# Self-attention layers of a four-layer transformer kernel: tied transposes, 4 KB pieces, later products, and one pair in eight transposed by TensorE

## The chip, the cores and the metric

The kernel runs on one core of a Trainium2 chip. That core has five engines which work side by side, each through its own list of instructions, strictly in order: TensorE (PE; its loads of weights are listed apart as PEld), VectorE (DVE), ScalarE (ACT), GpSimd (POOL) and SyncE (SP), which mostly issues DMAs. The metric is the device time of one execution in microseconds. Lower is better.

## The reference

x is (4, 1024, 256): four items of 1024 tokens with 256 channels, all in fp32. Four layers follow one another: L0 (16 heads: self-attention, cross-attention to a context of 77 tokens, feed-forward), L1 (three attention blocks of 4 heads with 64 channels each), L2 and L3 (16 heads, cross-attention). The change concerns the second and third blocks of L1, where queries, keys and values all come from x. Cut to what matters:

```python
Q = relu(q @ Wq + bq);  K = relu(k @ Wk + bk);  V = relu(v @ Wv + bv)   # (4,1024,256), 4 heads of 64
scores = einsum('hbqd,hbkd->hbqk', Qh, Kh) / sqrt(64)                   # 1024 x 1024 for each head
scores = where(key_mask == 0, NEG, scores)
attn = softmax(scores, axis=-1) * query_mask
out = layer_norm(einsum('hbqk,hbkd->hbqd', attn, Vh) + q)
enc = leaky_relu(out @ Wff + bff, 0.2) + out                            # q, k, v of the next block
```

## The kernel before

**Units.** The class Self4 computes such a block for one item. Two blocks times four items make eight items, and each has 16 units: p = 0, 1 (a pair of heads) times t = 0 to 7 (a tile of 128 queries). The 128 units fill 948 to 1902 us of the profiled execution, "the stage" here. One unit consists of the following.

- *Scores* (scores, L1262): four matmuls (eight records) of 64x512 give 128 queries x 1024 keys for each of two heads, in two PSUM tiles named ss. Their pool has two buffers, so a unit's ss tiles are the only ones: the next unit's scores can write only what this unit's exponentials have read.
- *Reductions* (L1273): VectorE takes the maximum over the keys, one reduction for each head.
- *Exponentials* (L1279): ScalarE writes exp(score - max) for both heads into a tile PR and sums it in passing. One PR holds a pair of units, that is two query tiles (t even, t odd). There are two PR buffers.
- *Block transposes* (turned_by_blocks, L1291): the products with V need the probabilities with keys on the partitions. VectorE transposes PR in place in blocks of 32x32, one instruction of 128x2048 for a unit. It is called one unit later (pipe.later("next", 1)).
- *The DMAs* (L1298): after the pair's second block transpose, 16 DMAs of 128 KB each move the blocks from PR to a tile PT, where the whole is transposed. Half is issued by SP (a = 0, 2), half by POOL (a = 1, 3); each DMA consists of runs of 1 KB. There are two PT buffers.
- *Products with V* (weighted, L1334): 16 matmuls of 128x256 for each half of the keys, called at ("turn", 2) and ("turn", 3): the first half two units after the DMAs were issued, the second half one unit after that. After the second half ScalarE copies the result from PSUM into OT (carry, L1512). For every four query tiles, OT is transposed back and normalized (normal, L1348).
- *A step of the pump*: work for the neighbouring items, spread evenly over the units. It consists of the heads of Q and K (L1226, L1231; evicted by ScalarE into QK, L1233), of V (values, L1187, L1190; evicted by ScalarE in L1194), of turns of x (L1167, L1396; copied by ScalarE, L1512), and of the feed-forward (L1402, L1405; ScalarE in L1410, then VectorE in L1411 and L1412).

**Order.** TensorE's order is written by hand: it is the order in which Pipe.unit calls the parts, and the call of a kind that was deferred ("full", "next", "turn", "late", "col") stands where its name stands there:

```python
        self.call("full")
        if scores:
            scores()
        self.call("next")
        self.now += cost
        self.pump()
        for kind in ("turn", "late", "col"):
            self.call(kind)
```

So TensorE does scores, step, products in each unit. The orders of the other engines are made when the kernel is built, by a planner that estimates when each instruction could start; `issue_after` ties an instruction behind a given one.

**Branches.** What the mask holds selects a branch at run time. In the branch that runs here `net.blocks` is true: PR and PT take two buffers of 16 KB a partition each, and `carry` is always a ScalarE copy.

## Time and profile before

| | us |
|---|---|
| median of 3 runs | 2405.5 |
| the three runs | 2398.03, 2405.5, 2406.79 |
| the profiled execution | 2396.79 |
| its span | 2394.9 |
| mean granted TensorE clock | 0.958 |
| the stage of the 128 units | 948 to 1902 |

The profiled execution is one run of the program; its time is the metric's, and its span runs from the first to the last instruction. In the profile's rows, L12 stands for line 12 of the kernel. A group row reads: line, engine, operation, written tile <- read tile, size, count, then busy time in us and mean ns of one, then the engine's idle time just before these instructions and what ended most of it. A row of waits reads: engine, tile and line that waited <- what it waited for: us in total, times, longest. A timeline row reads: start in us, length in us, engine, line, operation, tiles, size, count, and in brackets the idle time before and its releaser. PEclk and "clock" are the TensorE clock that was granted, as a share of full speed.

### The profile page before, as it was taken

How to read it: one execution, taken by the hardware profiler on the slowest of the kernel's cores; microseconds unless marked ns; L12 is line 12 of the kernel's file. 1: busy time of each engine (PE TensorE's matmuls, PEld its weight loads, DVE VectorE, ACT ScalarE, POOL GpSimd, SP SyncE). 2: the span in 40 equal slices, each digit the busy share in tenths (PEclk: the TensorE clock that was granted, in tenths of full speed). 3: DMA queues.
4: the chain of work that ended last, by engine and by line, in shares of the span. 5: the costliest groups of instructions: out<-in, count | busy, mean ns of one | idle time of the engine just before them, and what ended most of it. 6: DMA issues, size and time to landing. Idle time of an engine off the chain costs nothing. (4 is left out here: it accounts for less than half of the span.)

```text
span 2394.9 us, 31195 instructions
## 1 busy us (share of the span) xinstructions
PE 2204.3 (92%) x11035; PEld 1204.8 (50%) x11035; DVE 1582.6 (66%) x3167; ACT 930.2 (39%) x1828; POOL 380.4 (16%) x648
## 2 busy tenths in 40 slices
PE   6899999999898979999999899999999899999996
PEld 3565446566577655545454445454545344444442
DVE  6665553534424565888888788888888656656765
ACT  2222332222232355545454454444444234434333
POOL 2000000000000000333333233333333100000000
PEclk8999989989998998999999999999999899999988
DMA  5000010000000000667776577766787400000000
GB/s 147 1 3 14 5 36 1 1 3 5 12 1 7 1 5 1 146 147 152 151 156 144 123 151 157 151 142 141 148 163 143 97 5 1 5 1 1 27 18 28
DMA packets 148677, 158.01 MB, mean 66 GB/s; under 512 B 51432, under 2 KB 130849, under 8 KB 148513
## 3 DMA queue, kind: packets, MB, share of 16 engines
q1 hardware_dynamic: 122161, 85.63, 17.2%
q0 software_dynamic: 25296, 69.24, 13.1%
q8 instruction: 91, 1.49, 0.3%
q10 hardware_dynamic: 1056, 1.05, 0.1%
q14 instruction: 73, 0.60, 0.1%
HBM read 17.41 MB, written 4.19 MB: 9 GB/s over the span
## 5 line engine op out<-in xcount | busy, mean ns | idle before, releaser
L1279 ACT ACTIVATE PR<-ss,nm 128x1024 f32<-128x1024 f32 x256 | 284.7, 1114 | 366.2 <-DVE nm L1273 290.2
L1291 DVE STREAM_TRANSPOSE PR<-PR 128x2048 f32<-128x2048 f32 x128 | 295.8, 2311 | 128.9 <-ACT PR L1279 114.3
L1298 POOL DMA_DIRECT2D PT<-PR x512 | 279.6, 554 | 577.7 <-PE ss L1262 236.7
L1262 PE MATMUL ss<-QK 64*128 64x512 f32 x1024 | 324.8, 628 | 28.8 <-ACT PR L1279 28.5
L1273 DVE TENSOR_REDUCE nm<-ss 128x1 f32<-128x1024 f32 x256 | 299.6, 1210 | 13.8 <-PE ss L1262 13.8
L377 ACT ACTIVATE PT<-pb 77x1024 f32<-77x1024 f32 x192 | 185.4, 1015 | 193.2 <-PE pb L373 193.2
L1334 PE MATMUL po<-PT,V 128*64 128x256 f32 x2048 | 251.1, 387 | 5.1 <-DMA PT<-PR 5.1
L281 DVE TENSOR_REDUCE mx<-pa 128x4 f32<-128x308 f32 x384 | 161.4, 470 | 83.7 <-PE pa L276 82.5
L1262 PEld LDWEIGHTS ss<-QK 64*128 64x128 f32 x1024 | 113.3, 187 | 176.8 <-ACT PR L1279 99.7
L1334 PEld LDWEIGHTS po<-PT,V 128*64 128x64 f32 x2048 | 136.6, 137 | 108.4 <-issue 51.1
L276 PE MATMUL pa<-KA,QT 64*128 64x308 f32 x768 | 169.1, 486 | 14.0 <-DVE mx L281 12.8
L1545 POOL TENSOR_TENSOR pw<-va,minus_half 128x4 f32<-128x4 f32 (+1 forms) x28 | 38.8, 1384 | 714.5 <-DVE va L1543 542.0
L386 PE MATMUL po<-PT,Vc 77*32 77x512 f32 x768 | 140.4, 639 | 7.6 <-ACT PT L377 7.0
L276 PEld LDWEIGHTS pa<-KA,QT 64*128 64x128 f32 x768 | 84.3, 193 | 99.1 <-issue 37.0
L604 PE MATMUL pp<-hF,w 128*128 128x256 f32 x512 | 116.9, 382 | 0.0
L367 PE MATMUL pb<-QT,KA 32*77 32x512 f32 x768 | 114.1, 665 | 0.0
L619 PE MATMUL pp<-w,hid 128*128 128x256 f32 x512 | 113.7, 379 | 0.0
L619 PEld LDWEIGHTS pp<-w,hid 128*128 128x128 f32 x512 | 97.0, 190 | 16.5 <-issue 2.2
L604 PEld LDWEIGHTS pp<-hF,w 128*128 128x128 f32 x512 | 95.6, 190 | 18.2 <-issue 6.0
L266 PE MATMUL pp<-hT,wq 128*128 128x512 f32 x192 | 98.0, 646 | 5.5 <-ACT hT L1507 5.0
L1536 DVE BATCH_NORM_STATS2 st<-x 128x6 f32<-128x256 f32 x256 | 97.7, 403 | 3.2 <-DMA x<-in_x 2.3
L1405 PE MATMUL pp<-wo,hE 128*128 128x256 f32 x384 | 96.4, 393 | 1.6 <-ACT hE L1512 1.6
(256 smaller groups left out, 3079.5 us busy)
## 6 DMA issues: line engine op xcount, KB each, us to landing
PT<-PR SPq DMA_DIRECT2D x512, 128.0 KB
PT<-PR POOLq DMA_DIRECT2D x512, 128.0 KB, 4.9
x<-in_x SPq DMA_DIRECT2D x4, 1024.0 KB
out<-x SPq DMA_DIRECT2D x8, 512.0 KB
w<-in_ff_w SPq DMA_DIRECT2D x2, 1024.0 KB
gb<-in_norms POOLq DMA_DIRECT2D x5, 256.0 KB, 6.6
wk<-in_l_wk SPq DMA_DIRECT2D x10, 128.0 KB
wv<-in_l_wv SPq DMA_DIRECT2D x5, 256.0 KB
```

Of the source, the lines that this page charges most:

```text
L276: nc.tensor.matmul(pas[i], self.qt[rows, e, ts(t, P)], self.ka[rows, e, :, :], start=True, stop=True)
L281: nc.vector.tensor_reduce(out, pas[i].rearrange("p (j s) k -> p j s k", s=2), AX.X, ALU.max, negate=True)
L377: nc.scalar.activation(pt[:, 2 * i : 2 * i + 2, :], pbs[i][:SC], AF.Exp, scale=self.l.scale)
L386: nc.tensor.matmul(po[ts(j, h.slot), :], l.v[:, self.b, col : col + h.vw], pt[:, j, :], start=True, stop=True)
L604: nc.tensor.matmul(pp[:, i, :], self.w1[:, cc, ts(f + i, P)], s["hT"][:, cc, ts(q, 2 * P)], start=cc == 0, stop=cc == NC - 1)
L619: nc.tensor.matmul(pp[:, u, :], s["a"][:, f, ts(u, P)], self.w2[:, f, :], start=f == 0, stop=f == NF - 1)
L1262: nc.tensor.matmul(ss[h][:, k, :], self.qk[p][rows, 0, ts(t, P)], self.qk[p][rows, 1, ts(k, 512)], start=True, stop=True,)
L1273: nc.vector.tensor_reduce(self.nm[:, t, at], s2, AX.X, ALU.max, negate=True)
L1279: nc.scalar.activation(out, s2, AF.Exp, bias=self.nm[:, t, at], accum_out=self.sums[:, t, at])
L1291: nc.vector.transpose(part, part)
L1298: (nc.sync, nc.gpsimd)[a % 2].dma_start(out=pt[ts(c, 32), :, :, a].rearrange("p t h k j -> p (t h) (k j)"), in_=pr[ts(a, 32), :, :, ts(c, ...
L1334: nc.tensor.matmul(po[64 * h : 64 * h + 64], self.v[:, k, 64 * (2 * p + h) : 64 * (2 * p + h) + 64], pts[:, :, h, :, k, :] if net.blocks e ...
```

## The change

Four edits in Self4, all for the branch in which `net.blocks` is true.

1. Each block transpose is tied behind the later reduction of the scores issued last (`net.reduced`), which is the second reduction of the next unit.
2. PR and PT get another layout, so that each of the 16 DMAs moves runs of 4 KB in place of 1 KB. POOL issues the DMAs with a = 3 alone, SP those with a = 0, 1, 2.
3. The products with V move from ("turn", 2 + half) to ("next", 3 + half): a unit later, and ahead of the unit's pump step, so that TensorE does scores, products, step.
4. The pair of units with p = 1 and t = 2, 3 of each item (one pair in eight) skips the block transposes and the DMAs. Its probabilities are written in plain order, and `turned` transposes them on TensorE: 16 transposes of 128x128 for each of the two units, both sets called in one unit, with a ScalarE copy (carry) of 128x512 from PSUM to PT after every four.

```diff
--- before.py
+++ after.py
@@ -1263,22 +1263,27 @@
                     ss[h][:, k, :], self.qk[p][rows, 0, ts(t, P)], self.qk[p][rows, 1, ts(k, 512)],
                     start=True, stop=True,
                 )
+        blocks = net.blocks and (p, t // 2) != (1, 1)
         if not net.blocks:
             pr = net.tile("E", [P, 2, S], name="PR")
         elif t % 2 == 0:
-            self.pr = net.tile("E", [P, 2, 2, S], name="PR")
+            self.pr = net.tile("E", [P, 4, 2, 2, S // 4], name="PR")
+        if net.blocks and not blocks:
+            pr = self.pr.rearrange("p c t h n -> p (c t h n)")[:, ts(t % 2, 2 * S)].rearrange("p (h n) -> p h n", h=2)
         for h in range(2):
             at = slice(2 * p + h, 2 * p + h + 1)
             s2 = ss[h].rearrange("p k n -> p (k n)")
-            nc.vector.tensor_reduce(self.nm[:, t, at], s2, AX.X, ALU.max, negate=True)
-            if net.blocks:
-                out = self.pr[:, t % 2, h, :].rearrange("p (c k i) -> p k c i", c=4, i=32)
+            net.reduced = nc.vector.tensor_reduce(self.nm[:, t, at], s2, AX.X, ALU.max, negate=True)
+            if blocks:
+                out = self.pr[:, :, t % 2, h, :].rearrange("p c (k i) -> p k c i", i=32)
                 s2 = s2.rearrange("p (k c i) -> p k c i", c=4, i=32)
             else:
                 out = pr[:, h, :]
             nc.scalar.activation(out, s2, AF.Exp, bias=self.nm[:, t, at], accum_out=self.sums[:, t, at])
-        if net.blocks:
+        if blocks:
             net.pipe.later("next", 1, lambda pr=self.pr: self.turned_by_blocks(p, t, pr))
+        elif net.blocks:
+            net.pipe.later(("next", "turn")[t % 2], 2 - t % 2, lambda: self.turned(p, t, pr))
         else:
             net.pipe.later("full", 1, lambda: self.turned(p, t, pr))
 
@@ -1287,21 +1292,22 @@
 
         net = self.net
         nc = net.nc
-        part = pr[:, t % 2].rearrange("p h s -> p (h s)")
-        nc.vector.transpose(part, part)
+        part = pr[:, :, t % 2].rearrange("p c h n -> p c (h n)")
+        with net.tc.issue_after(net.reduced.ins):
+            nc.vector.transpose(part, part)
         if t % 2 == 0:
             return
 
-        pt = net.tile("B", [P, 2, 2, 4, NT, 32], name="PT")
+        pt = net.tile("B", [P, 4, 2, 2, NT, 32], name="PT")
         for c in range(4):
             for a in range(4):
-                (nc.sync, nc.gpsimd)[a % 2].dma_start(
-                    out=pt[ts(c, 32), :, :, a].rearrange("p t h k j -> p (t h) (k j)"),
-                    in_=pr[ts(a, 32), :, :, ts(c, 256)].rearrange("p t h n -> p (t h) n"),
+                (nc.gpsimd if a == 3 else nc.sync).dma_start(
+                    out=pt[ts(c, 32), a].rearrange("p t h k j -> p (t h k j)"),
+                    in_=pr[ts(a, 32), c].rearrange("p t h n -> p (t h n)"),
                 )
         state = []
         for half in range(2):
-            net.pipe.later("turn", 2 + half, lambda half=half: self.weighted(p, t, pt, half, state))
+            net.pipe.later("next", 3 + half, lambda half=half: self.weighted(p, t, pt, half, state))
 
     def turned(self, p, t, pr):
 
@@ -1315,25 +1321,26 @@
                 pm = net.p1.tile([P, 4, P], F32, tag="p1", name="pm")
                 for i in range(4):
                     nc.tensor.transpose(pm[:, i, :], pr[:, h, ts(k + i, P)], net.ident)
-                net.evac(pts[:, t % 2, h, k : k + 4, :], pm)
+                net.carry(pts[:, t % 2, h, k : k + 4, :], pm)
         if t % 2:
             state = []
             for half in range(2):
-                net.pipe.later("col", half, lambda half=half: self.weighted(p, t, pts, half, state))
-
-    def weighted(self, p, t, pts, half, state):
+                when = ("next", 3 + half) if net.blocks else ("col", half)
+                net.pipe.later(*when, lambda half=half: self.weighted(p, t, pts, half, state, False))
+
+    def weighted(self, p, t, pts, half, state, blocks=True):
         net = self.net
         nc = net.nc
         if half == 0:
             state.append(net.p1.tile([P, 2, P], F32, tag="p1", name="po"))
         po = state[0]
-        if net.blocks:
+        if blocks:
             po = po.rearrange("p t (a j) -> p t a j", a=4)
         for k in range(4 * half, 4 * half + 4):
             for h in range(2):
                 nc.tensor.matmul(
                     po[64 * h : 64 * h + 64], self.v[:, k, 64 * (2 * p + h) : 64 * (2 * p + h) + 64],
-                    pts[:, :, h, :, k, :] if net.blocks else pts[:, :, h, k, :], start=k == 0, stop=k == NT - 1,
+                    pts[:, :, :, h, k, :].rearrange("p a t j -> p t a j") if blocks else pts[:, :, h, k, :], start=k == 0, stop=k == NT - 1,
                 )
         if half:
             if t % 4 == 1:
```

## The prediction

> **What bounds the kernel now.** First the page's engine totals and slices, then the self-layer stage alone, then who waits for whom in it, then single units. "Scores", "products", "exponentials" and "step" are used as above; s is the start of a unit's first scores matmul.

> ```profile
> PE 2204.3 (92%) x11035; PEld 1204.8 (50%) x11035; DVE 1582.6 (66%) x3167; ACT 930.2 (39%) x1828; POOL 380.4 (16%) x648
> L1279 ACT ACTIVATE PR<-ss,nm 128x1024 f32<-128x1024 f32 x256 | 284.7, 1114 | 366.2 <-DVE nm L1273 290.2
> L1291 DVE STREAM_TRANSPOSE PR<-PR 128x2048 f32<-128x2048 f32 x128 | 295.8, 2311 | 128.9 <-ACT PR L1279 114.3
> q1 hardware_dynamic: 122161, 85.63, 17.2%
> q0 software_dynamic: 25296, 69.24, 13.1%
> ```

> The windows view for 948 to 1902 us (columns: length; busy us of PE, PEld, DVE, ACT, POOL; clock; DMA share; GB/s), then the waits:

> ```profile
> 948.00:1902.00 954.00, 901.14 (x4382) 444.31 (x4380) 789.16 (x1023) 446.73 (x912) 300.59 (x536) 0.98 0.70 145
> ...
> PEld ss L1262 <- ACT PR L1279: 99.7, 127, 2.4
> ...
> PE ss L1262 <- ACT PR L1279: 28.5, 38, 2.1
> ACT PR L1279 <- DMA PT<-PR: 27.2, 8, 4.0
> ```

> TensorE is the engine in use (901 of 954), but a unit's scores need both PSUM tiles that the exponentials of the unit before read, and they wait for them in nearly every unit. The timeline of one late unit:

> ```profile
> 1636.86 2.74 PE L1262 MATMUL ss<-QK 64*128 64x512 f32 x8
> ...
> 1637.60 2.31 DVE L1291 STREAM_TRANSPOSE PR<-PR 128x2048 f32<-128x2048 f32 x1 [1.29 <-ACT PR L1279]
> ...
> 1641.13 2.35 DVE L1273 TENSOR_REDUCE nm<-ss 128x1 f32<-128x1024 f32 x2
> ...
> 1642.38 1.11 ACT L1279 ACTIVATE PR<-ss,nm 128x1024 f32<-128x1024 f32 x1 [4.33 <-DVE nm L1273]
> 1643.52 1.11 ACT L1279 ACTIVATE PR<-ss,nm 128x1024 f32<-128x1024 f32 x1
> 1643.64 3.11 PE L1262 MATMUL ss<-QK 64*128 64x512 f32 x8
> ```

> The block transpose stands on VectorE ahead of the next reductions and itself waits 1.29 us for the exponentials. So the reductions start at s+4.27 and the exponentials at s+5.52. The next scores begin at 1643.64, when the first exponential has released its tile, and stall for the second: their block takes 3.11 us instead of the 1.92 of undisturbed units. A late unit thus costs TensorE until the first exponential's start + 2.24 (both) + 0.14, as if the next scores began only there. Over the 128 units the scores block lasts 2.52 us on average, 0.60 too long (77 us), and gaps ahead of its first matmul add about 18: **95 us** of TensorE time lost to late exponentials, inside the ceiling 99.7 + 28.5 = 128 of the two waits.

> **The tie.** Each transpose moves behind both reductions of the next unit. Then reductions start with their scores (s+2.0 in undisturbed units), the first exponential at s+3.3, the second ends at s+5.5, and the transpose finds its data ready: its 114.3 us of waiting goes, and the 95 us with it. Bounds: nothing regained, or 128. I take 95, from the scores blocks themselves. What it delays: the transpose of a pair's second unit now ends at about s+6.7 of the next unit, and its 16 DMAs start there.

> **Products a unit later, ahead of the step.** TensorE's order in a unit was scores, step, products; it becomes scores, products, step. The matmuls are the same, so for TensorE alone it costs nothing, and the extra unit covers the later DMAs. But it moves the end of the step's matmuls back by a products half (1.88 us), to s+1.92+1.88+2.24 = s+6.0 (2.24: two matmuls and a row of heads, or values, or forward), in a step of two heads tiles to s+7.3. That matters through ScalarE, whose order is a planner's. In the instruction order of the changed kernel, ScalarE has the OT copy and the evictions of the **same unit's step ahead of the first exponential** in most units with t even, those where the exponentials open a new PR buffer; 163 evictions of work that TensorE does after the same scores lie so, in 54 units, against 46 in 39 units before. ScalarE runs in order, so the exponentials wait for the step they do not need. The trace of before shows what one such case does, in the ScalarE timeline, after scores at 1323.16:

> ```profile
> 1326.86 2.05 ACT L1512 COPY hT<-pt 128x512 f32<-128x512 f32 x4 [2.66 <-PE pt L1167]
> 1329.17 1.11 ACT L1279 ACTIVATE PR<-ss,nm 128x1024 f32<-128x1024 f32 x1 [0.26 <-DVE nm L1273]
> ...
> 1330.30 1.11 ACT L1279 ACTIVATE PR<-ss,nm 128x1024 f32<-128x1024 f32 x1
> ```

> There the exponential starts at s+6.0; the next scores began at s+7.27 and took 3.04 us, so they count from s+8.4, which is 6.0 + 2.38. In the changed kernel it is later: step end + 0.1 + eviction (0.68 for a QK tile, L1233; 0.47 for V, L1194), and 2.24 + 0.14 from there to the next scores, which TensorE spends idle: 0.1 + 0.68 + 2.38 = 3.16 us with a QK tile last, 2.95 with a V. I take 3.1. Counting the order, 33 units are so: positions 0, 2, 4, 6, 8 of the 16 in five of the eight items (25), and 8 units in the other three. 33 x 3.1 = **+102 us**. Eleven more even units have only the OT copy ahead (end of products s+3.8, + 0.1 + 0.37, + 2.38 = 6.65 against 5.9): 11 x 0.7 = **+8 us**. From below: were ScalarE's late evictions no worse than in before, 0; from above, two evictions after the last matmul, 4.0 each, 132.

> **The pair by TensorE.** In each of 8 items, 32 transposes of 128x128 in one unit: sixteen (L1167) ran from 1326.17 to 1328.09, 1.92 us, so 32 take 3.84 and eight times that is **+31 us** of TensorE, which has no cover. The PSUM copies, 8 of 128x512 (0.58 to 0.59 us, L1512), stand before the first exponential in six items, seven of them with another eviction: some 2.9 us beyond the unit's own TensorE work, 6 x 2.9 = **+17 us**. What goes: 16 block transposes (16 x 2.31 = 37 us of VectorE, which has 165 us idle in the stage, so nothing on the path) and 128 DMAs of 128 KB.

> The row here is 273 ns for one such transpose, 0.12 us when they follow each other. [...]

> **4 KB pieces, and 12 of 16 on SP.** Bytes are the same, packets a quarter. The software queue's 25296 packets cost 13.1% for 69.24 MB, the hardware queue's 122161 cost 17.2% for 85.63: per MB 0.189 against 0.201, so at most 6% of the transfers' time, and the DMA engines are not full (0.70). The queues: SP issues 8 in 8.06 us now, median 806 ns, so 12 take 9.7; POOL's 4 take 2.2 instead of 4.4. Landing is 4.9 (2.4 to 7.6). The chain that matters: transpose end, 9.7 + 2.4 to 4.9 = 12 to 14.6 us, then PR is free for the exponentials of the unit after next. Slow even units (two units: 16.5 us, s+8 in the next, less 6.7) leave 17.8 us, which hides it; quick ones (12.6 + 3.3 - 6.7 = 9.2) don't and wait 3 to 5. Six or seven even units are quick: against the 27.2 us that before waits, I add **+10 us**; ends: -27 if the wait vanishes, +48 if every quick pair and some products wait.

> [...]

> **Sum**, on the profiled execution (2396.8, span 2394.9): -95 + 102 + 8 + 31 + 17 + 10 = +73, so 2470. The runs shown lie between 2398.0 and 2406.8, their median 8.7 above the profiled one; I add a part of that: **2472**.

> **Rivals.**
> - *Faster: ScalarE's order does no harm.* If the evictions end before the data of the exponentials are ready, only -95 + 31 + 17 + 10 stay: 2360, up to 2393 with half the 95. For it: ScalarE is busy only 447 of 954, and before has late evictions at low cost. Against: the step's matmuls lie behind scores and products on TensorE, so its eviction cannot be ready before s+6.7. It decides when the 33 delays are under (95 - 31 - 17 - 8 - 10)/33 = 0.9 us each.
> - *No change:* delays of 1 us: -95 + 33 + 8 + 31 + 17 + 10 = +4, 2401 (2393 to 2417). The same row speaks against it.
> - *Milder loss:* delays of 1.5 to 2 us (50 to 66 in place of 102), if stalls that I charge apart overlap: 2418 to 2440.
> - *DMAs bind as well:* SP's 12 in a line make exponentials wait in every even unit, and products for PT: +10 becomes +48, so 2508; with a fifth of the 95 not regained, 2527. For it: the SP row. Against: the slow even units themselves give the DMAs time.

> **How the numbers follow.** Chances: forecast 0.58 (2440 to 2500), milder 0.15, DMAs 0.10, no change 0.06, faster 0.11. The bound between them is 0.5%, 12 us, about what this measurement can tell. Leaving out faster, no change and a few hundredths above: 2410 to 2530; the forecast's own range is 2440 to 2500.

> **What the profile after would show.** Tie right: VectorE's 114.3 us wait for ScalarE gone, reductions near s+2. ScalarE right: even units of 9 to 10.4 us beside odd ones of 6 to 6.5, TensorE's scores still waiting for exponentials, 100 us or more, and ScalarE idle until TensorE's pp, pv or po ahead of them. DMA: a wait of the exponentials for PT<-PR near 40 us if right, over 75 if that rival is. Pair: 256 transposes, 31 us. It is wrong if the even units come out near 7 us: then planned order and actual wait differ, and the gain of the tie decides.

## The result and the profile after

The changed kernel takes 2514.3 us (median of four runs, 2503.5 to 2518.6) against 2406.1 for the kernel before: a ratio of 1.045, with a 95% interval of 1.041 to 1.049. That is 108 us slower; 66 were forecast. The time lies inside the outer range of 2410 to 2530, but above the 2440 to 2500 that the forecast gave for itself; by its number alone the rival "DMAs bind as well" (2508) is nearer, so the trace has to decide. The profiled execution took 2518.55 us, with a span of 2516.8. The time went up in the stage of the 128 units: from the first scores of the first unit to those of the last it took 1053.5 us (946.5 to 2000.0) against 921.4 (948.2 to 1869.6), 132 more. Outside the stage the span is 10 us shorter.

The page of the changed kernel:

```profile
PE 2280.3 (91%) x11291; PEld 1246.8 (50%) x11291; DVE 1549.7 (62%) x3151; ACT 975.4 (39%) x1892; POOL 210.2 (8%) x360
...
q1 hardware_dynamic: 80689, 106.61, 17.1%
q0 software_dynamic: 11472, 31.47, 5.1%
...
L1262 PE MATMUL ss<-QK 64*128 64x512 f32 x1024 | 355.5, 694 | 86.9 <-ACT PR L1282 86.9
L1276 DVE TENSOR_REDUCE nm<-ss 128x1 f32<-128x1024 f32 x256 | 302.5, 1217 | 203.6 <-PE ss L1262 203.3
L1282 ACT ACTIVATE PR<-ss,nm 128x1024 f32<-128x1024 f32 x256 | 284.4, 1115 | 205.3 <-DVE nm L1276 202.2
...
L1297 DVE STREAM_TRANSPOSE PR<-PR 128x2048 f32<-128x2048 f32 x112 | 257.7, 2300 | 0.0
```

Here lines 1276, 1282, 1297, 1304, 1341 and 1519 hold the reductions, exponentials, block transposes, DMAs, products and `carry`. The block transposes wait for nothing any more (0.0 in place of 128.9), and VectorE has time to spare: its reductions now wait 203 us for the scores. But TensorE's scores wait longer for the exponentials than before. The waits of 946 to 2004 us say so, and what ScalarE does first:

```profile
PEld ss L1262 <- ACT PR L1282: 151.5, 105, 4.9
ACT OT L1519 <- PE po L1341: 147.7, 50, 4.7
...
PE ss L1262 <- ACT PR L1282: 86.9, 46, 4.5
```

151.5 + 86.9 = 238 us, where the kernel before had 128. ScalarE waits 147.7 us for products whose result it is to copy into OT, 50 times and up to 4.7 us, although that copy is urgent for nobody. The exponentials hardly wait for the DMAs any more: 1.9 us in two waits, where before had 27.2 us. One even unit shows both. First TensorE's timeline, then VectorE's reductions for this unit, then ScalarE's:

```profile
1605.88 1.99 PE L1262 MATMUL ss<-QK 64*128 64x512 f32 x8
1607.79 1.95 PE L1341 MATMUL po<-PT,V 128*64 128x256 f32 x16
1609.67 3.70 PE L1226 MATMUL pp<-hT,wq 128*128 128x512 f32 x8
1615.24 4.87 PE L1262 MATMUL ss<-QK 64*128 64x512 f32 x8 [1.87 <-ACT PR L1282]
1620.05 3.37 PE L1341 MATMUL po<-PT,V 128*64 128x256 f32 x16
```

```profile
1608.47 2.35 DVE L1276 TENSOR_REDUCE nm<-ss 128x1 f32<-128x1024 f32 x2
```

```profile
1609.79 0.37 ACT L1519 COPY OT<-po 128x256 f32<-128x256 f32 x1 [0.23 <-PE po L1341]
1611.69 0.69 ACT L1233 ACTIVATE QK<-pp,qk_bias 128x512 f32<-128x512 f32 x1 [1.53 <-PE pp L1226]
1613.41 0.69 ACT L1233 ACTIVATE QK<-pp,qk_bias 128x512 f32<-128x512 f32 x1 [1.03 <-PE pp L1226]
1614.00 1.11 ACT L1282 ACTIVATE PR<-ss,nm 128x1024 f32<-128x1024 f32 x1
```

The first maximum was ready at s+3.8 (its reduction began at s+2.60), and the exponential starts at 1614.00, s+8.12, right behind the second eviction of the unit's own step. TensorE has done its share at 1613.37 and idles for 1.87 us. What the prediction had not seen comes next: the following scores take 4.87 us, where 3.08 is the usual length of scores that wait for the second exponential, and the products 3.37 us in place of 1.95. The windows view of these two units (length, busy us of PE, PEld, DVE, ACT, POOL, granted clock, DMA share, GB/s) names the reason:

```profile
1605.88:1615.24 9.36, 7.49 (x33) 3.18 (x32) 7.11 (x12) 4.40 (x11) 1.62 (x4) 1.00 0.52 128
1615.24:1626.17 10.93, 10.93 (x34) 4.33 (x34) 4.67 (x3) 3.94 (x7) 0.31 (x1) 0.69 0.73 200
```

After the idle time TensorE is granted 0.69 of its clock on average over the unit. Counted over all units as length times (1 - granted clock), the stage loses 81.8 us in this way, and lost 13.6 before. TensorE stood idle for 1.3 us or more ahead of the scores of 43 units (8 before); in 27 of them (3 before) the unit then lost 1.7 to 3.4 us to the clock, 75 us together.

Which gaps were followed by a fall can be read from the trace. The granted clock in it changes only at points that lie a whole number of 3.413 us apart, and between them it is 1.00 or 0.50: of the 28 falls of the stage nine lasted 3.413 us, 18 twice and one three times as long. Here, cut at such points, are the stretch around the gap at 1613.37 and the fall behind it, and then the two stretches over which a later gap of 1.88 us, from 1748.12 to 1750.00, is spread; the clock stays up behind that one:

```profile
1612.74:1616.15 3.41, 1.54 (x4) 0.29 (x2) 0.35 (x2) 2.74 (x5) 1.93 (x4) 1.00 0.51 137
1616.15:1622.98 6.83, 6.83 (x21) 2.85 (x22) 4.05 (x3) 2.55 (x6) 0.00 (x0) 0.50 0.84 221
...
1745.86:1749.27 3.41, 2.27 (x6) 0.72 (x4) 1.93 (x1) 1.79 (x3) 0.90 (x2) 1.00 0.09 19
1749.27:1752.69 3.42, 2.69 (x8) 0.97 (x8) 0.42 (x1) 1.77 (x4) 1.03 (x3) 1.00 0.91 236
```

Of the stretches of 3.413 us of the stage at full clock, 28 were followed by a fall, and TensorE was busy for at most 0.59 of each (here 1.54 of 3.41). Of the 232 that were not followed by one, only four were as little busy. Of the 40 gaps of 1.4 to 2.1 us ahead of scores, 21 lay within one stretch, and all 21 were followed by a loss; a boundary cut the other 19 in two, and 3 of these were.

The stage as one window, to be held against the row of before (clock 0.98, DMA share 0.70):

```profile
946.00:2004.00 1058.00, 961.34 (x4525) 480.47 (x4527) 740.13 (x965) 486.58 (x967) 126.93 (x243) 0.92 0.46 111
```

### The profile page after: what moved, and what is told of

It is laid out like the page before. It is cut to its first block, busy times and chain, and to the rows that moved or that the text cites. A ratio compares the mean times of both kernels' runs of the same rounds, so it can differ in the third digit from the quotient of the medians.

```text
span 2516.8 us, 31061 instructions
## 1 busy us (share of the span) xinstructions
PE 2280.3 (91%) x11291; PEld 1246.8 (50%) x11291; DVE 1549.7 (62%) x3151; ACT 975.4 (39%) x1892; POOL 210.2 (8%) x360
## 3 DMA queue, kind: packets, MB, share of 16 engines
q1 hardware_dynamic: 80689, 106.61, 17.1%
## 5 line engine op out<-in xcount | busy, mean ns | idle before, releaser
L1262 PE MATMUL ss<-QK 64*128 64x512 f32 x1024 | 355.5, 694 | 86.9 <-ACT PR L1282 86.9
L1341 PE MATMUL po<-PT,V 128*64 128x256 f32 x2048 | 272.9, 413 | 1.1 <-DVE mx L281 1.1
L1297 DVE STREAM_TRANSPOSE PR<-PR 128x2048 f32<-128x2048 f32 x112 | 257.7, 2300 | 0.0
L1262 PEld LDWEIGHTS ss<-QK 64*128 64x128 f32 x1024 | 120.1, 204 | 243.1 <-ACT PR L1282 151.5
L1341 PEld LDWEIGHTS po<-PT,V 128*64 128x64 f32 x2048 | 145.8, 147 | 178.7 <-issue 120.0
L1304 POOL DMA_DIRECT2D PT<-PR x224 | 109.4, 494 | 911.8 <-DVE st L1543 204.9
L619 PEld LDWEIGHTS pp<-w,hid 128*128 128x128 f32 x512 | 97.0, 190 | 16.5 <-issue 2.2
```

Source lines behind the costliest of these rows:

```text
L619: nc.tensor.matmul(pp[:, u, :], s["a"][:, f, ts(u, P)], self.w2[:, f, :], start=f == 0, stop=f == NF - 1)
L1262: nc.tensor.matmul(ss[h][:, k, :], self.qk[p][rows, 0, ts(t, P)], self.qk[p][rows, 1, ts(k, 512)], start=True, stop=True,)
L1297: nc.vector.transpose(part, part)
L1341: nc.tensor.matmul(po[64 * h : 64 * h + 64], self.v[:, k, 64 * (2 * p + h) : 64 * (2 * p + h) + 64], pts[:, :, :, h, k, :].rearrange("p a ...
```

## The experiments

The theory: ScalarE's order makes the exponentials of even units late, and TensorE idles; the clock then falls and makes it worse. The rivals: the PR buffers and their DMAs bind anyway; the clock falls for a reason of its own; one of the other three edits costs the time by itself. The ratios are against the kernel before, with 95% intervals.

| run | median us | ratio | interval |
|---|---|---|---|
| the changed kernel | 2514.3 | 1.045 | 1.041 to 1.049 |
| scalar_tied | 2429.8 | 1.012 | 1.004 to 1.020 |
| scalar_tied_no_pair | 2419.7 | 1.008 | 1.004 to 1.012 |
| products_back | 2448.0 | 1.018 | 1.008 to 1.029 |
| filler | 2514.9 | 1.045 | 1.037 to 1.054 |
| filler2 | 2493.4 | 1.037 | 1.030 to 1.044 |
| tie_only | 2445.6 | 1.018 | 1.009 to 1.028 |
| pieces_only | 2455.4 | 1.023 | 1.013 to 1.032 |
| products_only | 2392.8 | 0.997 | 0.993 to 1.000 |
| pair_only | 2416.4 | 1.005 | 1.002 to 1.009 |
| order_dve | 2396.2 | 0.998 | 0.995 to 1.001 |
| order_norm_dve | 2417.2 | 1.006 | 1.004 to 1.008 |
| tie_even | 2357.4 | 0.981 | 0.976 to 0.986 |

### ScalarE's order put right: scalar_tied

```diff
+    def behind(self):
+        return self.tc.issue_after(self.exp.ins) if self.blocks and self.exp else nullcontext()
     def carry(self, out, src):
         if self.blocks:
-            self.nc.scalar.copy(out, src)
+            with self.behind():
+                self.nc.scalar.copy(out, src)
...
-            nc.scalar.activation(out, s2, AF.Exp, ...)
+            net.exp = nc.scalar.activation(out, s2, AF.Exp, ...)
```

The evictions of V, QK and low are wrapped in `behind` in the same way.

> The changed kernel with one thing more: the OT copy, the PT copies and the evictions of the pump step on ScalarE are tied behind the exponentials of the unit that issued last. Theory (ScalarE's order idles TensorE, and the clock falls after the idle time): the first exponential of an even unit starts near s+3.3 instead of 6.7 to 10, the granted clock of the stage goes back from 0.92 to 0.98 or more, and the time falls by about 102 + 8 + 17 + 68 = 195, to 2320 to 2360, below the kernel before. Rival (the PR buffers and their DMAs bind anyway, ScalarE's order only fills the wait): the exponentials wait for PT<-PR 3 to 5 us in every even unit, 150 us or more in all, and the time stays above 2430.

Measured: 2429.8 us, 85 less than the changed kernel, and not the 150 or more that the theory wanted. ScalarE's order costs most of the loss: with it put right, about 23 us of the 108 remain. But the clock of the stage came back only to 0.96, not to the 0.98 of the theory (35.8 us are lost to it, 81.8 in the changed kernel, 13.6 before), and the first exponential of even units starts at s+5.2 on average (6.6 in the changed kernel), not at s+3.3. The rival held a part of the truth too. In the waits of 947 to 1916 us,

```profile
ACT PR L1284 <- DMA PT<-PR: 116.3, 25, 12.1
```

stands where the changed kernel had 1.9 us: the DMAs had been hidden behind the evictions and are the next thing that is late. Tying ScalarE's copies also did harm in one place. In the units where TensorE transposes, the PSUM copies now stand behind the exponentials, the exponentials behind the DMAs, and TensorE runs out of PSUM tiles:

```profile
1530.30 1.53 PE L1325 MATMUL pm<-ident,PR 128*128 128x128 f32 x12
1535.14 0.66 PE L1325 MATMUL pm<-ident,PR 128*128 128x128 f32 x4 [3.31 <-ACT OT L1527]
```

The ScalarE timeline at that place has the cause:

```profile
1532.53 1.11 ACT L1284 ACTIVATE PR<-ss,nm 128x1024 f32<-128x1024 f32 x1 [2.93 <-DMA PT<-PR]
```

### The same without TensorE's transposes: scalar_tied_no_pair

```diff
-        blocks = net.blocks and (p, t // 2) != (1, 1)
+        blocks = net.blocks
```

> As scalar_tied, but all pairs go by block transposes and DMAs, none by TensorE. Theory (TensorE is the bound once the exponentials are on time, and the 256 transposes have no cover): 31 us less than scalar_tied, 2290 to 2330. Rival (the DMAs' chain is then close, and the pair gives it air): the same as scalar_tied or up to 30 us more.

Measured: 2419.7 us, 10 less than scalar_tied, which is within the intervals of the two; both expectations missed. The exponentials still wait for the DMAs, 108.4 us in 26 waits. So the pair on TensorE makes little difference here. That the DMAs which start behind the tied transposes are what keeps both runs above the kernel before is likely from these waits, but no run takes the tie alone out of this order.

### The products back behind the step: products_back

```diff
-            net.pipe.later("next", 3 + half, lambda half=half: self.weighted(p, t, pt, half, state))
+            net.pipe.later("turn", 2 + half, lambda half=half: self.weighted(p, t, pt, half, state))
```

> The changed kernel with the products with V back after the pump step, two and three units after the DMAs were issued. TensorE's order is scores, step, products again, so the step's matmuls end 1.88 us earlier. Theory: the evictions ahead of the exponentials end 1.88 us earlier, even units lose 1.2 instead of 3.1 us, the idle time after them shrinks and the clock stays up; but the products may wait for PT, since the DMAs now start 6.7 us into a unit: 2400 to 2460. Rival (the place of the products does not matter, the tie delays the DMAs): 2490 to 2530.

Measured: 2448.0 us, 66 less than the changed kernel, as expected. ScalarE's order still has 146 evictions of the same unit's work ahead of exponentials, and the first exponential of even units comes only 0.4 us earlier on average (s+6.20 for 6.63), where 1.88 were expected. What changed more is TensorE: with the products behind the step it has work while the evictions run. It idles for 1.3 us or more ahead of the scores of 3 units in place of 43, and the stage loses 27.3 us to the clock in place of 81.8. In exchange the products wait 28.7 us for PT, 13 times. So the move ahead of the step was what made the late evictions dear in the changed kernel.

### Work for TensorE in the idle time: filler and filler2

```diff
     def scores(self, p, t):
...
+        if net.blocks and 8 * p + t in {(1, 0): (5, 9), (1, 3): (1, 3, 11), (2, 3): (1, 3, 9)}.get((self.l.n, self.b), (1, 3, 5, 7, 9)):
+            idle = net.p1.tile([P, 512], F32, tag="p1", name="idle")
+            for _ in range(4):       # 2 in filler2
+                nc.tensor.matmul(idle, net.ident, self.qk[p][:, 0, 0:512], start=True, stop=True)
```

> The changed kernel with four matmuls of 128x512 (about 1.88 us, written to a PSUM tile that nobody reads, so the result is the same) on TensorE ahead of the scores in the 33 units that follow a delayed even unit. No other work is moved. Theory (the idle time of 1.8 to 2.1 us before the scores lets the granted clock fall for 3.4 or 6.8 us): the clock of the stage rises from 0.92 to 0.97 or more, the scores blocks of 4.3 to 4.8 us go back to 3.0, and the time falls by 50 to 70, to 2445 to 2465. Rival (the clock falls for another reason, for example the mean load of the chip): clock unchanged, time 2510 to 2520 or more.

Measured: 2514.9 us, no change, although the clock of the stage rose from 0.92 to 0.96. The four matmuls took 3.5 us and not 1.88:

```profile
1616.50 3.60 PE L1261 MATMUL idle<-QK,ident 128*128 128x512 f32 x8
1620.02 1.99 PE L1266 MATMUL ss<-QK 64*128 64x512 f32 x8
```

Four matmuls leave eight records here, so the timeline row that I had taken for four matmuls (1.98 us, x4) holds two. Most of the units after them kept their clock (37.5 us are lost in the stage), and the filled units became about as much longer. So two matmuls were tried.

> As filler, but two matmuls of 128x512 in place of four: four took 3.5 us in filler, more than the idle time of 1.9 us that they were to fill, so that what the clock gave back went into longer even units. Two take about 1.75 us. Theory (the clock falls after the idle time, and its price is some 1.7 us for each fall): even units stay near 8.0 to 9.4 us, the clock of the stage 0.96 or more, and the time falls by 40 to 55 against the changed kernel, to 2460 to 2475. Rival (the clock is a symptom, the units last as long as the exponentials let them): 2505 to 2520.

Measured: 2493.4 us, 21 less than the changed kernel, though the intervals of the two overlap a little; in the profiled executions the stage is 31 us shorter (1022.2 against 1053.5) and the loss to the clock 30.6 us against 81.8. The same pair of units as above, with even unit and exponentials exactly as late as there (s+8.12):

```profile
1589.71:1599.08 9.37, 9.21 (x38) 3.95 (x37) 7.11 (x12) 4.40 (x11) 1.63 (x4) 1.00 0.65 136
1599.08:1606.78 7.70, 7.70 (x34) 3.21 (x34) 4.58 (x3) 3.86 (x7) 0.31 (x1) 1.00 0.92 247
```

Two matmuls that compute nothing of use shorten the odd unit from 10.93 to 7.70 us, because TensorE does not stand idle ahead of it. One such unit proves little, since some keep their clock without a filler; but over the stage the gaps of 1.3 us or more fell from 43 to 15, and those followed by a loss from 27 to 9. That the clock falls after the idle time is shown; the gain is half of what was expected. The loss to the clock fell by 51 us and the stage by only 31. Part of the difference can be seen: ScalarE's order came out a little worse with the two matmuls (174 early evictions in place of 163), and units such as the eleventh of the fifth item start their exponentials at s+6.72 in place of 4.44.

### Each edit alone on the kernel before: tie_only, pieces_only, products_only, pair_only

tie_only:

```diff
-        nc.vector.transpose(part, part)
+        with net.tc.issue_after(net.reduced.ins):
+            nc.vector.transpose(part, part)
```

> The kernel before with the tie alone: each block transpose behind both reductions of the next unit; old layout, 8 and 8 DMAs, products after the step, no pair on TensorE. ScalarE's order changes with it: 84 evictions of the same unit's step lie ahead of the exponentials, in 53 units (46 in 39 before); as the step comes ahead of the products here, each costs about 1 us, not 3.1. Theory (the tie removes the late reductions, but hands the time to late exponentials and to PR buffers that come free later): 2390 to 2430. Rival (the tie is good in itself and only the other parts cost): 95 us less than before, 2310 to 2340.

Measured: 2445.6 us, 39 more than before; the forecast of this run missed by 16. The reductions of odd units start at s+2.4 on average in place of 3.5, as the tie wants. But in even units the first exponential moved from s+4.95 to 5.70, and the waits of 955 to 1921 us show products and exponentials both waiting for the DMAs, which the tied transposes release later. ScalarE's order also changed in this run (84 early evictions in place of 46), and the two causes can't be told apart in it:

```profile
PE po L1335 <- DMA PT<-PR: 51.8, 24, 5.2
ACT PR L1279 <- DMA PT<-PR: 50.3, 20, 6.7
```

pieces_only (the layout, its access patterns, and `(nc.gpsimd if a == 3 else nc.sync)`):

```diff
-            self.pr = net.tile("E", [P, 2, 2, S], name="PR")
+            self.pr = net.tile("E", [P, 4, 2, 2, S // 4], name="PR")
...
-                (nc.sync, nc.gpsimd)[a % 2].dma_start(
-                    out=pt[ts(c, 32), :, :, a].rearrange("p t h k j -> p (t h) (k j)"),
-                    in_=pr[ts(a, 32), :, :, ts(c, 256)].rearrange("p t h n -> p (t h) n"),
+                (nc.gpsimd if a == 3 else nc.sync).dma_start(
+                    out=pt[ts(c, 32), a].rearrange("p t h k j -> p (t h k j)"),
+                    in_=pr[ts(a, 32), c].rearrange("p t h n -> p (t h n)"),
```

> The kernel before with the 4 KB pieces and the 12 to 4 split of the DMAs alone. 139 evictions of the same unit's step then lie ahead of exponentials, in 90 units. Theory (ScalarE's order, and SP's 12 issues in line, cost 0.5 to 1 us in each pair or unit): 2420 to 2470. Rival (only transfers change, and they are hidden): 2400 to 2412.

Measured: 2455.4 us, 49 more, though the transfers themselves got better (median landing 3.9 us in place of 4.9). The planner's order of ScalarE changed with the layout: 139 early evictions in 90 units, and the first exponential of even units starts at s+6.25 on average in place of 4.95. It is not SP's longer line of issues: the list of waits has none of the exponentials for PT<-PR. The block transposes wait 140.0 us for ScalarE, where before had 114.3.

products_only:

```diff
-            net.pipe.later("turn", 2 + half, lambda half=half: self.weighted(p, t, pt, half, state))
+            net.pipe.later("next", 3 + half, lambda half=half: self.weighted(p, t, pt, half, state))
```

> The kernel before with the products moved alone (a unit later and ahead of the step). 38 evictions of TensorE work after the scores lie ahead of the exponentials, 27 of them OT copies, in 35 units. Theory (the move does harm only through the evictions of a step that now ends later; here few are ahead of the exponentials): 2390 to 2425. Rival (the place of the products by itself costs the 3 us in the even units): 2470 or more.

Measured: 2392.8 us, a ratio of 0.997 whose interval ends at 1.000: no harm, perhaps a gain of some 10 us. The move is dear only where the evictions of the step stand ahead of the exponentials.

pair_only:

```diff
+        blocks = net.blocks and (p, t // 2) != (1, 1)
...
+        elif net.blocks:
+            net.pipe.later(("next", "turn")[t % 2], 2 - t % 2, lambda: self.turned(p, t, pr))
```

with the `turned` and `weighted` of the change, the products at ("turn", 2 + half).

> The kernel before with one pair in eight transposed by TensorE alone, its copies by ScalarE. Theory: TensorE pays 31 us, the PSUM copies of each batch hold up the exponentials or wait for PSUM tiles (2 to 3 us in each of 8 items, 20), VectorE is relieved of 37 us of transposes, of which part comes back since late reductions cost here: 2420 to 2450. Rival (VectorE's relief outweighs it): under 2400.

Measured: 2416.4 us, 10 more than before and just under the range, where TensorE alone pays 31. VectorE's relief, which the prediction costed at nothing, probably gave part of that back: without the tie the reductions are late, and in 16 units no block transpose stands ahead of them (those of odd units start at s+3.15 on average in place of 3.47).

The four differences add up to 39 + 49 - 14 + 10 = 84 us, and all four together cost 108. The two dear edits are those after which the planner puts more of ScalarE's evictions first. Much of their price is clock: in the profiled executions tie_only's stage is 41 us longer than before and loses 30 us more to the clock (43.8 in place of 13.6), that of pieces_only 59 and 27 (41.0).

### VectorE's other work moved in place of the transposes: order_dve, order_norm_dve

```diff
-            nc.vector.tensor_reduce(self.nm[:, t, at], s2, AX.X, ALU.max, negate=True)
+            with net.behind(net.block):          # the latest block transpose
+                reduced = nc.vector.tensor_reduce(self.nm[:, t, at], s2, AX.X, ALU.max, negate=True)
...
-        step.f()
+        with self.net.behind(self.net.reduced), self.net.behind(self.net.exp):
+            step.f()
```

`net.exp` is left unset here, so that only VectorE's order is changed; the block transposes are called ahead of the next scores ("full", 1), and the products are moved as in the change. The VectorE work of `normal` is tied behind the reductions in the same way. In order_norm_dve the VectorE part of `normal` is called one unit later as well.

> As order_norm_dve, but the normalization's VectorE part is called where it was, so it can stand between a block transpose and the next reductions. Theory: in one unit of four the normalization's 2.1 us delay the reductions; between products_only and order_norm_dve: 2340 to 2390. Rival (the normalization is not in the way): the same as order_norm_dve within 5 us.

> The kernel before (old layout, 8 and 8 DMAs, no pair on TensorE) with the products moved, and with VectorE's other work out of the way in place of the transposes: the block transpose stays ahead of the next reductions, and the normalization and the VectorE work of the pump step are tied behind the reductions, the normalization's VectorE part called a unit later. Theory (late exponentials cost TensorE up to 95 us, and what makes the reductions late is the transpose together with other VectorE work ahead of them): reductions start at s+2.0 to 2.6 instead of 3.5 on average, PR is not freed later, and the time falls by 30 to 90 against the kernel before, to 2315 to 2375. Rival (the transpose alone keeps the reductions late): within 15 us of products_only, 2380 to 2410.

Measured: 2396.2 and 2417.2 us. Both theories fell: order_dve is products_only again, and the later normalization costs another 21 us, so that the rivals' times missed too. Reductions still start at s+3.0 to 3.3 on average, and in order_dve the transposes still wait 104.3 us for the exponentials (114.3 before). So the transpose that waits for late exponentials seems to keep the next reductions late even with the other work out of its way, which is the rival's mechanism. In the profiled executions the stage of order_norm_dve is 25 us longer than that of order_dve, and 22 of these are lost clock (44.4 in place of 22.2); why its TensorE idles more was not followed up.

### Half of the tie: tie_even

```diff
-        nc.vector.transpose(part, part)
+        with net.tc.issue_after(net.reduced.ins) if t % 2 == 0 else nullcontext():
+            nc.vector.transpose(part, part)
```

on products_only.

> The kernel before with the products moved and half of the tie: only the block transposes of t even, behind which no DMA waits, are tied behind the reductions of the next unit; those of t odd stay where the planner puts them, and so do the DMAs and PR's release. Old layout, 8 and 8 DMAs, no pair on TensorE. ScalarE's order has 30 evictions of the same unit ahead of exponentials, 24 of them OT copies, in 27 units. Theory (a tie is worth having where nothing waits for the transpose): reductions of odd units start at s+2.0 to 2.3, those of even units near s+3.0, ScalarE waits for PT<-PR under 40 us, and the time falls by 10 to 40 against products_only, to 2350 to 2385. Rival (the two transposes in a row only move the lateness to the even units): 2385 to 2410.

Measured: 2357.4 us, a ratio of 0.981 (0.976 to 0.986) to the kernel before, and 35 less than products_only: faster than both kernels of this study. The stage, first to last scores, takes 890.0 us in place of 921.4. The page's row of the transposes and the waits of 952 to 1846 us:

```profile
L1292 DVE STREAM_TRANSPOSE PR<-PR 128x2048 f32<-128x2048 f32 x128 | 288.6, 2288 | 0.0
```

```profile
PEld ss L1262 <- ACT PR L1279: 72.7, 89, 2.7
```

The transposes wait for nothing, as with the full tie. The exponentials' wait for PT<-PR falls to 8.3 us (27.2 before), and the scores' wait for the exponentials from 99.7 to 72.7 in this row. The odd units' reductions start at s+2.45 on average (3.47 before), the even ones' at 3.20 (3.60). The block transpose of t even has no DMA behind it, and here its delay shows no cost; that of t odd has sixteen. A full tie with nothing but the products moved was not run. So of the 88 us between tie_only and tie_even it is not shown how much is the other half of the tie, how much the products' move, and how much ScalarE's order (30 early evictions in place of 84).

## Why the prediction was right, and where it was not

**ScalarE ahead of the exponentials (+102 and +8): right, in place and size.** With a QK tile last, s+6.7 or, for two heads tiles, s+8.1 were forecast for the first exponential by the prediction's rule; units of positions 2 and 0 show 6.72 and 8.12, those with V last 7.20 and 6.67, and those with OT alone 4.44. The delay of one such unit is 1.87 us of idle TensorE and 3.01 - 1.92 = 1.09 inside the next scores, 2.96 in all, where 3.1 was taken. scalar_tied confirms the cause: 85 us vanish with that order, lost clock included.

**The tie (-95): the reductions moved as told, the gain was less.** The transposes' wait went to 0.0, reductions start at s+2.4 and 2.7 on average (even and odd units), and quiet units run in 6.03 us. But tie_only costs 39 us: the step that failed is to credit the tie with all 95 and charge its delayed DMAs with 10. Where the evictions do not hide the DMAs, the exponentials wait 50 us for them and the products 52 in tie_only (where the products keep their old place), and the exponentials 116 in scalar_tied. How much of the 95 came in the changed kernel itself is not shown.

**The DMAs (+10): the sign was wrong in the changed kernel.** The wait of 27.2 us fell to 1.9, because the exponentials were later still; the lower end that the prediction had named (-27) is nearly what came. The rival with the DMAs as second bound did not take place there, and came into view only when ScalarE's order was mended.

**4 KB pieces: costed at too little, without effect on the sum.** The prediction allowed 6% of the transfers' time, by comparing two queues that both carried mixed sizes. Per MB the share of the span times the span is 17.2% x 2394.9 / 85.63 = 4.8 us before and 17.1% x 2516.8 / 106.61 = 4.0 us after on the hardware queue, 16% less. pieces_only, which moves the same bytes as before, has 19.5% x 2452.6 / 119.20 = 4.0 there too, and on the software queue 5.8% x 2452.6 / 35.67 = 4.0, where before had 13.1% x 2394.9 / 69.24 = 4.5. An issue on SP took 591 ns (median) in place of 806, but twelve in a row still took 8.6 us, where 9.7 had been taken:

```profile
1194.29 8.61 SPq L1304 DMA_DIRECT2D PT<-PR  x12
```

The same bytes thus took 12% to 17% less engine time in runs four times as long. It did not matter for the time, since the transfers were hidden: the exponentials of the changed kernel waited 1.9 us for them.

**The pair on TensorE (+31 and +17): about right.** The 256 transposes ran at 273 ns each, as in the row of before, and the units with them last 11.3 us, with exponentials at s+10.0 in the five items where copies stand ahead. Against a quiet unit that is 5.28 us, and 1.09 inside the next scores make 6.4, where 3.84 + 2.9 = 6.7 was forecast; the lost clock behind it comes on top. That VectorE's relief is worth nothing fits the changed kernel (it waits 203 us for scores); without the tie, the 10 us of pair_only suggest that it gives back some 20 of the 31.

**What was missing: the clock.** The sum has no term for it. The loss to the granted clock grew by 68 us in the stage, and that is more than the whole distance between the forecast of +73 and the +122 of the profiled execution. The stage without it would be 132 - 68 = 64 us longer, against 73 forecast; the 10 us that the rest of the span gained were not forecast either. How the remaining terms share those 64 us can't be split more finely from these runs. That the time still lies inside the outer range is in part luck: the missing 68 us were offset in part by the 9 and the 10. The trace of before had the price: eight of its units began after 1.3 us or more of idle TensorE, three of them lost 10 us to the clock together. At 10/8 = 1.25 us for each, the 33 delayed units and 6 of the batches that the prediction counted would have been another 49 us, and the forecast 2521 in place of 2472. The row to look at is the clock of single units right behind a stall, not the stage's average of 0.98.

The size of the loss follows from the falls: 1.7 or 3.4 us are lost where the clock stands at 0.50 for 3.4 or 6.8 us, and the row of 1616.15 shows 0.50 for 6.83 us. Gaps of 1.4 to 2.1 us were followed by a loss in 24 of 40 cases, so in this trace the length of a gap alone does not tell whether one follows.

**The rivals.** Faster and no change are ruled out by the even units; the milder loss by the 2.96 us; the DMAs, though their 2508 is nearest to the measured time, by the 1.9 us that the exponentials wait for them. (The "2393 with half the 95" of the first rival does not follow from its terms, which give -48 + 31 + 17 + 10 = +10, so 2407; nothing rests on it.) The direction of all this was set by the instruction order of ScalarE, which the diff does not show at all.

## What to carry to other kernels

When an edit delays the release of a buffer, look at what the planner then puts ahead of the instruction that waits for it: on an engine that runs in order, work that seems to fill a wait can become the wait (163 early evictions here, and 85 us less with their order put right). Tie first the instructions whose results nobody awaits; half of this change's tie, with the products' move, made the kernel 1.9% faster, while the whole tie by itself made it slower. Charge every new idle gap of TensorE twice, once for its length and once for the clock behind it (here a loss of 1.7 to 3.4 us after 27 of 43 gaps of 1.3 us or more), and take that price from single units of the trace.
